# Softmax begun inside the position network, weights loaded early into one room, and layer 1's gathers re-timed, in a four-layer vision kernel

## The chip, the cores and the metric

One core of a Trainium2 chip runs the whole program. TensorE (PE) multiplies; VectorE (DVE), ScalarE (ACT) and GpSimd (POOL) do the rest; SyncE (SP) issues most of the transfers and POOL the gathers. Each engine takes its own instructions strictly in order. The metric is the device time of one execution in microseconds (us). [...]

## What is computed

Two images `x` of 512 channels and 32 x 32 pixels go through four layers, all in float32:

```
# layer 0: attention with 64 sampled keys a group, and a position network
off  = tanh(pw(gelu(dwconv6x6(q)))) * 4           # 8x8 sampling offsets
kv   = grid_sample(xn, grid + off);  k, v = kw(kv), vw(kv)
bias = w3 . relu(w2 . relu(w1 . signed_log(pos)))  # for each query, key
attn = softmax(q k^T / 8 + bias)                   # 8 groups, 1024 x 64
x    = x + out_w(attn v);   x = x + mlp_w2 gelu(mlp_w1 bn(x))
# layer 1: deformable 3x3 convolution as a gate
d    = instance_norm(pw(dwconv3x3(x1)));  off = conv3x3(d)
dc   = deform_conv(d, off)                         # 9 taps, bilinear
x    = x * (d * sigmoid(layer_norm(dc))) + x * g(channel pools of x2)
# layer 2: linear attention;  x = x + gamma * Q (K V) / norm
# layer 3: group norm, attention of 8 heads over 1024 pixels, projection
x    = x + w_out(softmax(q k^T / 8) v)
```

## The kernel before

`layers` runs the stages one after the other, and weaves neighbours together with Python generators: a `yield` is a place where another stage's instructions may be put. PE's instructions stay in the order in which the program issues them (`manual_schedule`); the order on DVE, ACT, POOL and SP is made by the scheduler of the Tile framework. Tiles come from pools of a fixed number of buffers; a new tile in a buffer waits for the last reader of the old one, and so do pools that come to lie where a closed pool lay.

**Layer 0.** `queries_keys_values` ends with the queries in `q_pad`, keys in `kbd`, values in `vbd`. `biased_scores` (L755 to 885) runs the position network for eight pairs of groups, four of each image, two keys at a time: `hidden` (L794, L803) makes the first layer on DVE and ACT, `second_layer` issues matmuls of 32 columns in four column tiles (L814) with their evictions `lo` and `hi` on ACT (L824, L826) and a sum on DVE (L827), and `last_layer` (L835) adds keys into a score tile `sim`, one step behind. At the sixteenth key `scores` adds q times k; `store` (L857) copies a finished pair to `simT`. The score matrices thus sit transposed in `simT`.

`softmax_values` (L888) takes one image. Of each of its four pairs it transposes the scores (L899, pt), takes the maximum, subtracts (L905, L907, DVE), the exponential (L908, ACT), the sum, its reciprocal, the product (L910 to L912, DVE); `values` transposes back (L918, pb) and copies to SBUF (L924, `at`, ACT); `product` multiplies by the values (L930, po) and copies to `simT` (L933, DVE). Before the change image 0's runs alone on PE after the position network, with four two-bank PSUM tiles. `project` (L949) follows, then `Mlp.run(0)`, into which image 1's softmax is woven, and `project` for image 1.

**MLP.** `run` (L984) does two halves of 512 pixels in 16 steps each, ph (L1016), gelu on ACT (L1024), acc (L1005) two steps behind; `acc` is added to `x_all` on DVE (L1033). Its weights of 4 MB each and out_w are loaded when the pools of the position network have closed.

**Layer 1.** Beside `Mlp.run(1)` image 0's features are made (`Features`): x_pad copies on ACT (L1074), nine depthwise steps dw on DVE (L1082, L1086) for each of two halves, a channel gate, pd, then offsets. `Products` makes nine tap tables: 72 tiles of 8 matmul halves each (L1281, py), copied on ACT (L1289, y, four buffers) and written to DRAM by SP (L1290, `table<-y`). `Samples` gathers, for each tap and 128 pixels, the four neighbours (1 MB a tile, two indirect transfers on POOL, L1333) and adds them, weighted, in four DVE instructions (L1344, dfacc). `due` takes a tile when its tap's table is whole. `pools` is the ring of gather buffers; its length also says how many gathers run ahead of the additions. `FOUND` and `MADE` set which MLP step issues what.

After the MLP the rest of image 0's products goes with image 1's features and more of image 0's sums (`sums0`), then image 1's 72 products with: the last of `sums0`, image 0's gate (`gate_image`), image 1's sums (`sums1`), and from the gate on `Linear.run(0)` (layer 2: pqk, pv L1455, v L1463, pkv L1448, pa L1514) and `group_norm_terms` (pm, pvar L1554), one step of these for each product. Then h is normalized (L1612), keys and queries of image 0 are computed (L1652, pq), image 1's gate is woven into their end, and `Linear.run(1)` is woven with `att.values(0)` (32 matmul steps, pv L1629).

**Layer 3.** `heads` (L1705 and after) makes logits (L1719, pl), a maximum (L1807, DVE), an exponential (L1815, ACT), transposes (L1769, pt) and weighted sums (L1734, po) for 64 pieces of work, with one piece ahead, and fills gaps with other steps (`fill`).

## Time and profile before

| what | us |
|---|---|
| median of 3 runs | 4014.14 (4012.45 to 4018.51) |
| the profiled execution's own time | 4015.97 |
| its span, first to last instruction | 4014.2 |
| PE busy in the span | 3895.0 (97%) |
| DVE, ACT, POOL busy | 2980.4, 2530.8, 339.3 |
| mean granted PE clock | 0.992 |
| transfers in the span | 274.39 MB |
| idle on DVE's sums, waiting for gathers | 214.0 in 92 waits |

A stage can be found by its windows on PE: 73.3 us busy in the first 100 us, 8.99, 11.41 and 16.37 us busy in 2100 to 2120, to 2140 and to 2160 (softmax of image 0; clock 0.90, 0.76, 0.83; DMA share 0.76, 0.50 and 0), 92.97 in 2900 to 3000, 96.03, 92.73, 97.05 and 91.83 in the four hundreds that follow, and 31.64 in the 40 us from 3480 on (start of the heads). In the slices of the page each digit is a tenth of busy time in 100.4 us; PEclk is the granted clock. In rows by time the first number is the start and the second the length from first to last of the group (xcount); in brackets stands the idle time of the engine just before, and what ended it. A float32 matmul shows as two instructions. In the list of waits the three numbers are the total, how many, and the longest.

### The profile page before, as it was taken

Reading aid. Unit: us, or ns where it says so; the run is one execution under the profiler, and the core shown is the slowest. Engines: PE = TensorE matmul, PEld = TensorE weight load, DVE = VectorE, ACT = ScalarE, POOL = GpSimd, SP = SyncE. Lnnn points to the kernel's source line nnn. Section 1 sums busy time; section 2 is a strip of 40 time slices with the busy share of each in tenths; the row PEclk is TensorE's granted clock in tenths of the full one; section 3 lists DMA queues with packets and bytes.
Section 4 is the critical chain, followed back from the end, with each engine's and each line's share of the span. In section 5 each row is a group of like instructions: output and inputs, shape, how many; then the busy total and the mean of one; then the engine's idle time right before and its main releaser. Section 6 shows DMA issues by size and latency. Waiting matters only on the chain. (4 is left out here: it accounts for less than half of the span.)

```text
span 4014.2 us, 59880 instructions
## 1 busy us (share of the span) xinstructions
PE 3895.0 (97%) x25548; PEld 1499.3 (37%) x25548; DVE 2980.4 (74%) x3326; ACT 2530.8 (63%) x2848; POOL 339.3 (8%) x325
## 2 busy tenths in 40 slices
PE   7999999999999999999997999999999999999999
PEld 4322222222222222222323444444434344355555
DVE  7999999999999999999983104054768677466665
ACT  7999999999999999999991112111112112155544
POOL 0000000000000000000000000033445343000000
PEclk9999999999999999999998999999999999999999
DMA  3000000000000000000002000166779685000000
GB/s 105 8 15 22 22 22 1 22 22 22 22 1 22 22 22 22 1 22 22 1 9 97 0 0 24 36 217 222 271 268 366 233 325 186 0 1 11 1 19 24
DMA packets 90479, 274.39 MB, mean 68 GB/s; under 512 B 9140, under 2 KB 10804, under 8 KB 86884
## 3 DMA queue, kind: packets, MB, share of 16 engines
q0 software_dynamic: 42432, 154.39, 11.0%
q1 hardware_dynamic: 47780, 116.18, 8.0%
q8 instruction: 200, 3.28, 0.3%
q14 instruction: 67, 0.55, 0.0%
HBM read 228.33 MB, written 42.21 MB: 67 GB/s over the span
## 5 line engine op out<-in xcount | busy, mean ns | idle before, releaser
L814 PE MATMUL ph<-h,w_t 128*32 128x512 f32 x16384 | 1796.0, 593 | 15.5 <-ACT lo L824 7.1
L794 DVE TENSOR_TENSOR h<-ab 128x1024 f32<-128x1024 f32 x1024 | 1206.4, 1220 | 73.5 <-PE ph L814 72.5
L814 PEld LDWEIGHTS ph<-h,w_t 128*32 128x32 f32 x16384 | 530.2, 110 | 1255.9 <-issue 1072.8
L803 ACT ACTIVATE h<-h 128x1024 f32<-128x1024 f32 x832 | 870.0, 1065 | 46.2 <-DVE h L794 43.4
L827 DVE SCALAR_TENSOR_TENSOR hi<-lo,low_w,hi 128x1024 f32<-128x1024 f32 x512 | 655.4, 1280 | 30.0 <-ACT hi L826 29.3
L826 ACT ACTIVATE hi<-ph,size_b,size 128x1024 f32<-128x1024 f32 x512 | 620.1, 1211 | 15.3 <-PE ph L814 9.5
L824 ACT ACTIVATE lo<-ph,vec_t 128x1024 f32<-128x1024 f32 x512 | 570.9, 1115 | 2.4 <-PE ph L814 2.4
L1344 DVE SCALAR_TENSOR_TENSOR dfacc<-got,wts,dfacc 128x512 f32<-128x512 f32 x560 | 409.3, 749 | 210.6 <-DMA got<-table,idx 198.2
L1281 PE MATMUL py<-dc_w_t,d 128*128 128x512 f32 x1152 | 515.5, 601 | 21.2 <-ACT y L1289 21.0
L1289 ACT COPY y<-py 128x512 f32<-128x512 f32 x144 | 83.5, 584 | 502.2 <-PE py L1281 424.4
L1333 POOL DMA_INDIRECT got<-table,idx x288 | 318.6, 1106 | 516.3 <-DVE dfacc L1344 157.6
L1281 PEld LDWEIGHTS py<-dc_w_t,d 128*128 128x128 f32 x1152 | 217.4, 192 | 302.0 <-issue 266.6
L1815 ACT ACTIVATE e<-pl,m 128x1024 f32<-128x1024 f32 x128 | 143.5, 1121 | 226.2 <-DVE m L1807 226.2
L1807 DVE TENSOR_REDUCE m<-pl 128x1 f32<-128x1024 f32 x128 | 150.8, 1220 | 144.5 <-PE pl L1719 144.5
L835 PE MATMUL sim<-hi,w 128*32 128x512 f32 x2048 | 244.8, 592 | 1.8 <-DVE hi L827 1.8
L1016 PE MATMUL ph<-xn,mlp_w_t 128*128 128x512 f32 x512 | 229.6, 593 | 0.0
L1005 PE MATMUL acc<-h,mlp_w_t 128*128 128x512 f32 x512 | 229.4, 592 | 0.0
L1024 ACT ACTIVATE h<-ph,vec_t 128x512 f32<-128x512 f32 x64 | 44.0, 687 | 254.2 <-PE ph L1016 254.0
L1069 POOL MEMSET x_pad<- 128x1156 f32 x2 | 2.2, 1094 | 2061.9 <-PE ph L814 2061.9
L1769 PE MATMUL pt<-cst_t,e 128*128 128x128 f32 x1024 | 147.8, 277 | 5.8 <-ACT aT L1780 3.0
L1769 PEld LDWEIGHTS pt<-cst_t,e 128*128 128x128 f32 x1024 | 117.6, 141 | 92.6 <-issue 61.2
L1005 PEld LDWEIGHTS acc<-h,mlp_w_t 128*128 128x128 f32 x512 | 97.3, 190 | 121.9 <-issue 121.6
(228 smaller groups left out, 2536.9 us busy)
## 6 DMA issues: line engine op xcount, KB each, us to landing
table<-y SPq DMA_DIRECT2D x144, 256.0 KB
ab<-feat_d SPq DMA_DIRECT2D x64, 512.0 KB
dc_w_t<-in_dc_w_dram SPq DMA_DIRECT2D x18, 1024.0 KB
mlp_w_t<-in_mlp_w_dram SPq DMA_DIRECT2D x2, 4096.0 KB
got<-table,idx POOLq DMA_INDIRECT x288
w_qkv_t<-in_w_qkv_dram SPq DMA_DIRECT2D x3, 1024.0 KB
out_dram<-x_all SPq DMA_DIRECT2D x12, 256.0 KB
x_all<-in_x_dram SPq DMA_DIRECT2D x4, 512.0 KB
```

The costliest lines, as they stand in the source:

```text
L794: nc.vector.tensor_tensor(h1, at_x[:, k : k + 1, :].to_broadcast([128, 32, 32]), at_y[:, k, :].unsqueeze(2).to_broadcast([128, 32, 32]), A ...
L803: nc.scalar.activation(h1, h1, AF.Relu)
L814: nc.tensor.matmul(ph[32 * t : 32 * t + 32, half(n)], lhsT=w2[:, c0 : c0 + 32], rhs=pair[t // 2][:, half(n)], start=True, stop=True, skip_ ...
L824: nc.scalar.activation(lo, phs[0], AF.Relu, bias=b2_lo)
L826: nc.scalar.activation(hi, phs[1], AF.Relu, bias=size_b, scale=size)
L827: nc.vector.scalar_tensor_tensor(hi, lo, low_w, hi, ALU.mult, ALU.add)
L835: nc.tensor.matmul(sim[32 * t : 32 * t + 32, half(n)], lhsT=w3[:, 30 - j : 62 - j], rhs=sums[t][:, half(n)], start=(j == 0), stop=(j == 30 ...
L1005: nc.tensor.matmul(accs[oc], lhsT=self.w2[:, m, 128 * oc : 128 * oc + 128], rhs=hs[m], start=(m == 0), stop=(m == 15),)
L1281: nc.tensor.matmul(py, lhsT=f.d[:, cc, 128 * c : 128 * c + 128], rhs=w[:, cc, :], start=(cc == 0), stop=(cc == CC - 1),)
L1333: nc.gpsimd.indirect_dma_start(out=g[:, 2 * dy : 2 * dy + 2, :].rearrange("p s c -> p (s c)"), out_offset=None, in_=self.products.tables[f ...
L1344: self.net.nc.vector.scalar_tensor_tensor(acc, g[:, s, :], self.f.wts[:, c, k, s : s + 1], self.f.bias if (k, s) == (0, 0) else acc, ALU.mult,
L1769: nc.tensor.transpose(pt[:, 128 * c : 128 * c + 128], e[:, 128 * k : 128 * k + 128], ident)
```

## The change

It has six parts.

1. **Room.** `q_pad` becomes the first use of one tile, `room`, of 128 x (4 x 2048 + 2048) floats. After the scores of the last pair the room is taken again, for out_w and the first MLP weight, which `load_weights` loads from there on. `kbd` and `w2` move to a pool of their own. The second MLP weight is loaded where it was.
2. **Softmax of image 0** is called inside `biased_scores`. Its first two steps (transposes, maximum, subtraction and exponential, sum, product of pairs 0 and 1) are issued before the last `last_layer`; the rest comes after it, and the store of pair 7 last. Its PSUM tiles come from the position network's three, its e and at from the buffers of h1 and hi. For image 0 the copy of the product to `simT` goes to ACT instead of DVE.
3. **End of the MLP.** `sums0` has three buffers instead of two, and in MLP steps 30 and 31 no tile of `sums0` is issued.
4. **Layer 1.** The further pool `df_more` has one buffer instead of two. Image 1's features start after the second product. `sums1` has two buffers until image 0's gate is done, and then four more; it had three, and two more from that gate to product 62. The gate takes two steps for each product, Linear and group norm one in two of three products.
5. **Values of image 0.** Only as many steps run beside `Linear.run(1)` as that has; the remaining ones run in `heads` between the first logits and the first transposes, in banks of layer 3.
6. `h1` is a flat tile; `turn` takes a pool and a tag.

Context lines are cut where they do not matter.

```diff
@@ -280,7 +280,8 @@
     def turn(name):
-        return banks["turn"].tile([128, 512], F32, name=name, tag="turn")
+        pool, tag = banks["turn"]
+        return pool.tile([128, 512], F32, name=name, tag=tag)
     bn = 1.0 / math.sqrt(1.0 + 1e-5)
@@ -291,44 +292,64 @@
         vbd = sim_pool.tile([128, NP, 128], F32, name="vbd", tag="vbd")
+        room = ExitStack()
+        big = net.pool(room, "l0_q")
+        def new_room():
+            return big.tile([128, 4 * 2048 + CC * C], F32, name="room", tag="room")
         with ExitStack() as l0a:
             l0a.enter_context(net.tc.manual_schedule(engines={mybir.EngineType.PE}))
-            big = net.pool(l0a, "l0_q")
-            q_flat = big.tile([128, (NP * 36 + 6) * 34], F32, name="q_pad", tag="q_pad")
+            q_flat = new_room()[:, : (NP * 36 + 6) * 34]
             q_pad = q_flat[:, : NP * 36 * 34].rearrange("p (n y x) -> p n y x", y=36, x=34)
-            kbd = big.tile([128, NP, 128], F32, name="kbd", tag="kbd")
+            keys = net.pool(l0a, "l0_k")
+            kbd = keys.tile([128, NP, 128], F32, name="kbd", tag="kbd")
             dram = net.pool(l0a, "cpb_dram", space=bass.MemoryType.DRAM)
             feat = dram.tile([32, 2048], F32, name="feat_d", tag="feat_d")
-            w2 = big.tile([128, 128], F32, name="w2_t", tag="w2")
+            w2 = keys.tile([128, 128], F32, name="w2_t", tag="w2")
             first = net.pool(l0a, "cpb_ab", 4)
...
             nc.sync.dma_start(out=w2, in_=net.ins["w2"])
-            biased_scores(net, q_pad, kbd, feat, w2, simT, first, parts)
+            def load_weights():
+                t = new_room()
+                w1 = t[:, : 4 * 2048].rearrange("p (k m) -> p k m", m=2048)
+                out_w = t[:, 4 * 2048 :].rearrange("p (k m) -> p k m", m=C)
+                nc.sync.dma_start(out=out_w, in_=net.ins["out_w"])
+                nc.sync.dma_start(out=w1, in_=net.ins["mlp_w1"])
+                return w1, out_w
+            w1, out_w = biased_scores(
+                net, q_pad, kbd, feat, w2, simT, vbd, first, parts, load_weights
+            )
         later.enter_context(net.tc.manual_schedule(engines={mybir.EngineType.PE}))
...
         image0 = ExitStack()
-        with ExitStack() as l0b:
-            mlp = Mlp(net, l0b, s2)
-            out_w = net.load("out_w", net.pool(scores, "out_w", side="right"))
+        with room, ExitStack() as l0b:
+            mlp = Mlp(net, l0b, s2, w1)
             soft = net.pool(scores, "att_tmp", 2, side="right")
-            with ExitStack() as ctx:
-                ps = net.psum(ctx, "att_ps", 4)
-                for _ in softmax_values(net, 0, simT, vbd, soft, ps):
-                    pass
             mlp.open_psum(l0b)
...
                 ps = net.psum(ctx, "att_ps1", 1)
+                def two_banks(name):
+                    return ps.tile([128, HW], F32, name=name, tag="two")
+                def one(name, size):
+                    return soft.tile([128, size], F32, name=name, tag=name)
                 project(net, 0, simT, out_w, mlp.bank)
-                weave(mlp.run(0), softmax_values(net, 1, simT, vbd, soft, ps), 1, 3)
+                weave(mlp.run(0), softmax_values(net, 1, simT, vbd, one, two_banks), 1, 3)
                 project(net, 1, simT, out_w, mlp.bank)
...
             with ExitStack() as ctx:
-                banks["turn"] = net.psum(ctx, "ft_ps", 2)
+                banks["turn"] = net.psum(ctx, "ft_ps", 2), "turn"
                 found = f0.run(turn, False)
@@ -336,18 +357,19 @@
                         some(found, 99)
-                        sums0 = Samples(net, f0, products, own0, 2, side="right")
+                        sums0 = Samples(net, f0, products, own0, 3, side="right")
                         taken = sums0.run()
...
                             next(made)
-                            if taken is not None:
+                            if taken is not None and i < 30:
                                 sums0.due(taken)
...
             kv_bank = net.bank(l1, "l2_kv")
-            banks["turn"] = net.psum(l1, "l1_y", 2)
+            banks["turn"] = net.psum(l1, "l1_y", 2), "turn"
             def bank(name):
@@ -357,39 +379,42 @@
             f1 = Features(net, 1, own1)
-            more = net.pool(own1, "df_more", 2)
-            sums0.pools += [more, more]
+            more = net.pool(own1, "df_more", 1)
+            sums0.pools += [more]
             found = f1.run(bank, True)
             for i, _ in enumerate(made):
-                some(found, 2)
+                if i > 1:
+                    some(found, 2)
                 if i % 4 < 3:
...
             sums1 = Samples(net, f1, products, own1, 1)
-            sums1.pools += [more, more]
+            sums1.pools += [more]
             tmp = net.pool(own1, "df_tmp", 1)
...
             taken1 = sums1.run()
-            aside = None
+            aside, ctx2 = None, None
             for i, _ in enumerate(made):
-                if i == 62:
-                    sums1.pools = sums1.pools[:3]
                 if aside is None:
...
                         wait = i + 4
-                else:
-                    sums1.due(taken1)
-                    if i >= wait and next(aside, None) == "gated":
-                        own0.close()
-                        ctx2 = ExitStack()
-                        extra = net.pool(ctx2, "df_extra", 2, side="right")
-                        sums1.pools += [extra, extra]
-                        linear.open(ctx2, side="right")
-                        aside = chain(
-                            linear.run(0, bank, kv_bank),
-                            group_norm_terms(net, linear.tmp, 0, bank),
-                        )
+                    continue
+                sums1.due(taken1)
+                if ctx2 is None and i >= wait:
+                    if next(aside) != "gated" and next(aside) != "gated":
+                        continue
+                    own0.close()
+                    ctx2 = ExitStack()
+                    linear.open(ctx2, side="right")
+                    extra = net.pool(own1, "df_extra", 4)
+                    sums1.pools += [extra] * 4
+                    aside = chain(
+                        linear.run(0, bank, kv_bank),
+                        group_norm_terms(net, linear.tmp, 0, bank),
+                    )
+                elif ctx2 is not None and i % 3 < 2:
+                    next(aside, None)
             for _ in aside:
@@ -409,9 +434,11 @@
                 linear.open(ctx)
-                weave(linear.run(1, bank, kv_bank), att.values(0, turn))
+                values = att.values(0, turn)
+                for _ in linear.run(1, bank, kv_bank):
+                    next(values)
             l2.close()
-        layer3(net, att, later, out)
+        layer3(net, att, later, values, banks, out)
@@ -752,7 +779,9 @@
     return done
-def biased_scores(net, q_pad, kbd, feat, w2, simT, first, parts):
+def biased_scores(net, q_pad, kbd, feat, w2, simT, vbd, first, parts, load_weights):
@@ -790,9 +819,9 @@
             k = 16 * (j // 32) + j % 16
-            h1 = hid1.tile([128, 32, 32], F32, name="h1", tag="h1")
+            h1 = hid1.tile([128, HW], F32, name="h1", tag="h1")
             nc.vector.tensor_tensor(
-                h1,
+                h1.rearrange("p (y x) -> p y x", x=32),
                 at_x[:, k : k + 1, :].to_broadcast([128, 32, 32]),
@@ -801,7 +830,7 @@
                 nc.scalar.activation(h1, h1, AF.Relu)
-            return h1.rearrange("p y x -> p (y x)")
+            return h1
         def second_layer(pair):
@@ -880,18 +909,34 @@
                 scores(p, sim)
+                if p == NP - 1:
+                    weights = load_weights()
             pending = (p, j, sums)
+        def two_banks(name):
+            return ps_h.tile([128, HW], F32, name=name, tag="ph")
+        def one(name, size):
+            if size == HW:
+                pool, tag = (hid1, "h1") if name == "e" else (highs, "hi")
+                return pool.tile([128, HW], F32, name=name, tag=tag)
+            return small.tile([128, size], F32, name=name, tag=f"soft_{name}", bufs=2)
+        soft = softmax_values(net, 0, simT, vbd, one, two_banks)
+        some(soft, 2)
         last_layer(sim, *pending[1:])
+        for _ in soft:
+            pass
         store(NP - 1, sim)
-def softmax_values(net, b, simT, vbd, tmp, ps):
+        return weights
+def softmax_values(net, b, simT, vbd, one, banks):
     nc = net.nc
     ident = net.cst("ident")
-    def banks(name):
-        return ps.tile([128, HW], F32, name=name, tag="two")
     def attention(p):
@@ -901,12 +946,12 @@
             )
-        m = tmp.tile([128, 16], F32, name="m", tag="m")
+        m = one("m", 16)
         nc.vector.tensor_reduce(m, pt, AX.X, ALU.max)
-        e = tmp.tile([128, 16, 64], F32, name="e", tag="e")
+        e = one("e", HW).rearrange("p (h j) -> p h j", j=64)
         nc.vector.tensor_tensor(e, pt, m.unsqueeze(2).to_broadcast([128, 16, 64]), ALU.subtract)
         nc.scalar.activation(e, e, AF.Exp)
-        s = tmp.tile([128, 16], F32, name="s", tag="s")
+        s = one("s", 16)
         nc.vector.tensor_reduce(s, e, AX.X, ALU.add)
@@ -920,7 +965,7 @@
             )
-        at = tmp.tile([128, HW], F32, name="at", tag="at")
+        at = one("at", HW)
         nc.scalar.copy(at, pb)
@@ -930,7 +975,8 @@
             )
-        nc.vector.tensor_copy(simT[:, p, :], po)
+        (nc.scalar.copy, nc.vector.tensor_copy)[b](simT[:, p, :], po)
     first = CC * b
@@ -967,12 +1013,12 @@
     LAG = 2
-    def __init__(self, net, ctx, s2):
-        self.net, self.s2 = net, s2
+    def __init__(self, net, ctx, s2, w1):
+        self.net, self.s2, self.w1 = net, s2, w1
         w = net.pool(ctx, "mlp_w")
...
         self.hp = net.pool(ctx, "mlp_h", self.LAG + 2)
-        self.w1, self.w2 = net.load("mlp_w1", w), net.load("mlp_w2", w)
+        self.w2 = net.load("mlp_w2", w)
     def open_psum(self, ctx):
@@ -1702,7 +1748,7 @@
         self.ps_o = net.psum(ctx, "l3_out", 1)
-    def heads(self, work, fill):
+    def heads(self, work, first, fill):
@@ -1750,6 +1796,8 @@
             self.divide(*e)
+        for _ in first:
+            pass
         for at, (b, hp, s0) in enumerate(work):
@@ -1823,7 +1871,8 @@
         return self.ps_t.tile([128, 512], F32, name=name, tag="pt3")
-def layer3(net, att, ctx, out):
+def layer3(net, att, ctx, values, banks, out):
     att.open_heads(ctx)
@@ -1859,7 +1908,8 @@
     ]
-    att.heads(first + second, fill)
+    banks["turn"] = att.ps_t, "pt3"
+    att.heads(first + second, values, fill)
     for _ in att.project(1, 768, 256, out, att.last_bank):
```

## Prediction

> **What bounds the kernel now.** I read the page first: busy time by engine, then the span in 40 slices.
>
> ```profile
> PE 3895.0 (97%) x25548; PEld 1499.3 (37%) x25548; DVE 2980.4 (74%) x3326; ACT 2530.8 (63%) x2848; POOL 339.3 (8%) x325
> ...
> PE   7999999999999999999997999999999999999999
> ...
> PEclk9999999999999999999998999999999999999999
> DMA  3000000000000000000002000166779685000000
> ```
>
> TensorE (PE) is the bound: 3895.0 of 4014.2 us, so only 119.2 us of the span are idle on it, and 26.7 of those lie in the first 100 us (73.3 us busy there), which the change leaves alone. At most about 92 us of gaps, and the slow matmuls after them, are open to it. No matmul is removed, so every gain has to be a gap. The second dip (slice 22, also in the clock) is the softmax of image 0; the DMA row shows where tables and gathers run. The waits of PE say who opens the gaps:
>
> ```profile
> PE py L1281 <- ACT y L1289: 21.0, 10, 8.7
> PE pb L918 <- DVE e L912: 14.1, 2, 9.0
> ...
> PE pq L1652 <- ACT h L1612: 7.3, 1, 7.3
> ...
> PE pkv L1448 <- DVE v L1463: 5.6, 2, 4.5
> ...
> PE pl L1719 <- ACT e L1815: 2.6, 1, 2.6
> ```
>
> (Total, number, longest.) Four of these five sit where the diff works; now each stage in time.
>
> **Softmax of image 0.** PE, start and length, wait in brackets; then the ACT load of the exponential's table:
>
> ```profile
> 2099.41 4.89 PE L814 MATMUL ph<-h,w_t 128*32 128x512 f32 x42
> ...
> 2110.32 1.94 PE L899 MATMUL pt<-cst_t,simT 128*128 128x128 f32 x16 [1.47 <-DVE simT L857]
> 2121.21 1.97 PE L918 MATMUL pb<-cst_t,e 128*128 128x128 f32 x8 [8.95 <-DVE e L912]
> 2124.27 3.78 PE L930 MATMUL po<-at,vbd 128*128 128x512 f32 x4 [1.10 <-ACT at L924]
> ...
> 2139.78 1.87 PE L918 MATMUL pb<-cst_t,e 128*128 128x128 f32 x8 [5.18 <-DVE e L912]
> ...
> 2152.03 3.27 PE L956 MATMUL po<-simT,out_w_t 128*128 128x512 f32 x7 [1.32 <-DVE simT L933]
> ```
>
> ```profile
> 2115.00 1.28 ACT L908 ACT_TABLE_LOAD   x1 [9.43 <-DVE e L907]
> ```
>
> From the last position-network matmul (2104.3) to the first of the projection (2152.0) go 47.7 us. DVE is the limit: maximum, subtract, sum and product of a pair take 1.22 us each, reciprocal 0.24, so about 5.1 us a pair. ACT: exponential 1.06, copy 1.01.
>
> The new order puts the 16 transposes of pairs 0 and 1 ahead of the last score matmuls, in banks that are free, with nothing between them and 2104.3. In us after 2100: pt0 to 5.4, pt1 to 6.4; DVE m0 to 6.7, the last hi (1.28, now behind m0) to 8.0; scores to 9.9; e0 to 9.2, m1 to 10.4; exponential 0 at 9.3 to 10.35, since the table load no longer waits for DVE and goes into ACT's idle time after the last hi (2105.6); s0 to 11.6, e1 to 12.8, reciprocal, the store of pair 7 (1.28) to 14.4, product of e0 to 15.6. pb0 starts at 15.7 instead of 21.2: a lead of 5.5, after a PE gap of 5.8. Then pb0 1.97, copy 1.1, po0 3.78, pt2 1.91, pb1 1.08 to 25.6. m2 waits for pt2; e2, exponential, s2, m3, e3 and the product of e2 follow to 33.8, so pb2 starts at 33.9 after a gap of 4.1 (before: 39.8 after 5.18). With pb2, po2 slow (1.87, 3.78) and pb3, po3 fast, plus copies, the projection starts at 46.1; with both fast (1.08, 1.98), at 43.4. The stores of the products move from DVE (1.23) to ACT (about 1.0): no loss. Gain 5.9 to 8.6.
>
> [...] The rows: after 8.95 us of waiting, pb, po and pt took 1.97, 3.78 and 1.91 against 1.08, 1.98 and 1.04 when warm, 3.56 us lost; after 5.18, 2.6 lost. [...] by the rows, 46.1 (gain 5.9). I take **7**.
>
> **The loads.** out_w (1 MB) and the first MLP weight (4 MB) overlay the queries after the scores of pair 7 at about 1980, on SP's queue: the last ab loads are already ahead of them, behind them stands only the second MLP weight, which still starts at 2104. The DMA row is 0 there. The projection waited for simT and not for the load, so this buys nothing by itself; it is worth 0 even without cover, because 5 MB are needed 120 us later. The second weight alone (4 MB; 313 GB/s were moved in 2100 to 2120, so 13 us) lands before 2120. Image 0's weights and POOL's clearing of x_pad now wait for the last e of the softmax (about 2134); behind them on SP and POOL stand only tables and gathers, which start over 200 us later (DMA row): 0.
>
> **End of the MLP.** Gathers (POOL), sums (DVE) and tables (PE, ACT, SP) meet here. PE, ACT, DVE and POOL rows:
>
> ```profile
> 2873.61 6.73 PE L1281 MATMUL py<-dc_w_t,d 128*128 128x512 f32 x11 [8.66 <-ACT y L1289]
> ```
>
> ```profile
> 2872.03 1.05 ACT L1074 COPY x_pad<-x_all 128x1024 f32<-128x1024 f32 x1 [10.83 <-DVE dw L1086]
> ```
>
> ```profile
> 2858.90 0.75 DVE L1344 SCALAR_TENSOR_TENSOR dfacc<-got,wts,dfacc 128x512 f32<-128x512 f32 x1 [3.82 <-DMA got<-table,idx]
> ```
>
> PE stood 8.66 us because the y copies are queued on ACT behind the second x_pad copy, that waits for nine DVE steps on the first, and these wait behind a sum whose gather is late. With 1.01 us just before and 1.6 of half clock (11 matmul halves in 6.73 us; 8 take 3.70), 11.3 us are at stake. The change asks for 5 gathers fewer in the last two MLP steps (62 for 72), gives the sums a third buffer, and starts image 1's features two products later: 10 products of 3.43 us stand ahead of the block instead of 9, 34 us, against a second x_pad copy that I put 27 to 32 us after the first product. The gap closes or shrinks to some us. The bias row b_q now stands on DVE ahead of 12 sums (9 us) and waits for the last hidden matmul, about 2822; they still end before the x_all additions at 2843.8, so hidden. Gain 0 to 11, I take **8**. The five tiles come later: 5 x 3.3 us (a tile's 1 MB at the DMA's full share) = 16 us more for the tail.
>
> **Layer 1 and 2 of image 0.** Linear work goes into two of three products instead of each, three products earlier; so 5 instead of 16 products are left after its last statistics. Gaps that this can close: 5.6 (v behind sums) and 1.9 (pvar). Gain 0 to 7, **4**. h no longer waits for gathers into the extra pool; but the 7.3 was the last table's write, which stays: **1**. Against it: image 1's sums have two buffers (three before) until the gate of image 0 is done, then six (five, three at the end). A tile then takes a gather (3.3) and four additions (3.0) in a two-deep ring; some 11 tiles at about 1 us more, with the 16 us above, less what six buffers win back while the table work flows more evenly. The sums ended at 3370.6; the gate of image 1 reaches PE at 3383.9, so some 9 us are free. Between -3 and +9, I take **+3**. The third projection weight (1 MB) now waits for the last gather instead of 3278; it is needed at about 3402, 28 us after 3370.6 + 3.3, and nothing behind it on SP is wanted before the heads: hidden.
>
> **Heads.**
>
> ```profile
> 3483.17 1.99 PE L1719 MATMUL pl<-qk 64*128 64x512 f32 x8
> 3487.76 4.41 PE L1719 MATMUL pl<-qk 64*128 64x512 f32 x8 [2.61 <-ACT e L1815]
> ```
>
> Thirteen value steps (26 halves of 0.44 = 11.5 us) move behind the first logits, over the first exponentials: the 2.61 and the 2.42 of half clock go. Here 2.6 us of idleness were already enough: [...] by the row it is 5.0, and the row decides. The first logits now wait up to 2 us for an addition. Gain 2 to 6, **4**.
>
> **Sum.** -7 - 8 - 4 - 1 + 3 - 4 = -21 against the profiled execution's 4015.97 (span 4014.2 and 1.8 around it): 3995; that execution lies 1.8 over the median of 4014.14, so **3993**.
>
> **Rivals.** (a) Layer 1 stays even: what leaves the MLP's end comes back as later stalls, and only softmax and heads count, -11: 4003. For it: DMA share 0.93 in 2840 to 2870, 0.92 in 3000 to 3100; fewer gathers early are more later. (b) All gaps close: 9 + 11 + 7 + 6 for h + 6 = -39: 3975. For it: all those waits are orders, not bandwidth; against it, h's is a write. (c) It does not do what it says: DVE's 5 us a pair still set the softmax (gain 3), and a new ACT queue before the products and the wait at the logits take most of the rest: about 4009. (d) Slower: the two-buffer ring and the deferred tiles delay the last sum of image 1, and the gate, then Linear, wait on PE one for one. It must eat 9 us of slack, the other gain of 24, and 8 more: 41 us, a dozen tiles at 3.3. For it: additions waited 214 us for gathers in all; a POOL issue took 8.67 us at 2865 while DVE ran without a gap. With 14 tiles (46 us) it is +13: 4027. Against it: POOL stood idle 34 and 24 us near 3201 and 3247 for want of tables, so the tail can catch up.
>
> **How the numbers follow.** Chances: the forecast 0.46 (own range 3984 to 4001), (a) 0.21, (b) 0.15, (c) 0.11, (d) 0.07. A difference of 0.2%, 8 us, is what a measurement can tell from none. Faster: the first three and a third of (c), 0.86; same: most of (c), 0.08; slower 0.06. The range leaves out the low half of (b), and (d): 3975 to 4010.
>
> **What would show it.** pb0 near 2115.7 and the projection at 2143 to 2146; ACT's table load at 2105.6; no wait over 4 us on y near 2873; pkv's wait under 2; second logits in 2 us after a value product. Wrong if PE waits for the gate of image 1; if y's waits move rather than go; or if the first pb still waits for DVE until 2119.

## The result, and the profile after

The changed kernel takes 4001.49 us (median of 6 runs, 3998.97 to 4007.06), the kernel before beside it 4016.29 (4012.45 to 4022.08): 14.8 us less, a ratio of 0.9964 (95% interval 0.9951 to 0.9977). Forecast were 21 us less. The sign, the place of two gains (softmax and heads) and the range were right; the end of the MLP was not.

Four marks on PE divide both profiled executions (4014.2 and 3999.3 us) into stretches that hold the same work: the end of the last position-network matmul, the first of the projection, the last one of the MLP (acc), the first one on h (pq).

| stretch, us | before | after | difference | forecast |
|---|---|---|---|---|
| start to the last position matmul | 2104.3 | 2103.8 | -0.5 | 0 |
| to the projection (softmax of image 0) | 47.7 | 39.4 | -8.3 | -7 |
| to the MLP's last matmul | 687.5 | 687.5 | 0.0 | 0 |
| to the first matmul on h (layer 1, Linear of image 0) | 497.0 | 496.4 | -0.6 | -10 |
| to the end (keys, gate, values, heads) | 677.7 | 672.2 | -5.5 | -4 |

Layer 1's -10 is the sum of -8, -4, -1 and +3 in the prediction. The waits of PE in the page of the changed kernel (total, number, longest):

```profile
PE py L1327 <- ACT y L1335: 26.3, 11, 8.2
...
PE pb L963 <- DVE e L957: 8.9, 2, 5.2
PE pq L1698 <- ACT h L1658: 7.9, 1, 7.9
...
PE pp L1254 <- DVE pos L1201: 4.9, 2, 4.7
```

The waits on v, on the group norm's terms and of the second logits, 5.6, 1.9 and 2.6 before, are gone from the list. The softmax's wait fell from 14.1 to 8.9. But y rose from 21.0 to 26.3, and pos from 0.2 to 4.9. In the order of time, the softmax on PE:

```profile
2103.74 1.97 PE L944 MATMUL pt<-cst_t,simT 128*128 128x128 f32 x16
...
2114.44 1.94 PE L963 MATMUL pb<-cst_t,e 128*128 128x128 f32 x8 [5.19 <-DVE e L957]
2117.48 3.78 PE L975 MATMUL po<-at,vbd 128*128 128x512 f32 x4 [1.10 <-ACT at L969]
2121.05 1.74 PE L944 MATMUL pt<-cst_t,simT 128*128 128x128 f32 x8
2122.64 1.04 PE L963 MATMUL pb<-cst_t,e 128*128 128x128 f32 x8
2124.77 1.98 PE L975 MATMUL po<-at,vbd 128*128 128x512 f32 x4 [1.10 <-ACT at L969]
2126.59 1.04 PE L944 MATMUL pt<-cst_t,simT 128*128 128x128 f32 x8
2131.34 1.09 PE L963 MATMUL pb<-cst_t,e 128*128 128x128 f32 x8 [3.71 <-DVE e L957]
2133.54 3.78 PE L975 MATMUL po<-at,vbd 128*128 128x512 f32 x4 [1.10 <-ACT at L969]
2137.11 1.91 PE L963 MATMUL pb<-cst_t,e 128*128 128x128 f32 x8
...
2143.21 7.13 PE L1002 MATMUL po<-simT,room 128*128 128x512 f32 x16 [1.10 <-ACT simT L979]
```

The transposes stand ahead of the scores, without a wait, and the two waits for e are still there, shorter. The table load went into ACT's free time: no wait in front of it, at 2105.10 and not at 2115.00.

```profile
2105.10 1.28 ACT L953 ACT_TABLE_LOAD   x1
```

The heads' start: the second logits run in 1.99 us, straight after 11.43 us of value steps.

```profile
3461.05 1.99 PE L1765 MATMUL pl<-qk 64*128 64x512 f32 x8
3462.97 11.43 PE L1675 MATMUL pv<-w_qkv_t,h 128*128 128x512 f32 x26
3474.33 1.99 PE L1765 MATMUL pl<-qk 64*128 64x512 f32 x8
```

The end of the MLP, PE and then ACT:

```profile
2842.43 17.43 PE L1327 MATMUL py<-dc_w_t,d 128*128 128x512 f32 x40 [1.41 <-ACT y L1335]
2868.10 16.63 PE L1327 MATMUL py<-dc_w_t,d 128*128 128x512 f32 x32 [8.24 <-ACT y L1335]
```

```profile
2840.84 1.05 ACT L1120 COPY x_pad<-x_all 128x1024 f32<-128x1024 f32 x1 [6.03 <-POOL x_pad L1115]
...
2866.52 1.05 ACT L1120 COPY x_pad<-x_all 128x1024 f32<-128x1024 f32 x1 [12.86 <-DVE dw L1132]
```

The wait that was to close is 8.24 us; it was 8.66. ACT stood idle for 12.86 us ahead of the x_pad copy, though PE waited for y from 2859.86 on, and began the two y copies queued behind it at 2867.47, right at its end: it took neither out of turn. The granted clock behind the wait was 0.50 here (2868.10 to 2872.00) and before (2873.61 to 2876.50). Count from the MLP's last matmul (2839.5 before, 2830.7 after): the second x_pad copy came at 32.5 before and comes at 35.8; eight products stand ahead of this wait, the block, instead of seven (24 + 40 halves against 48 + 8). A later wait in the same stretch, for the offsets' positions, grew as well:

```profile
2985.57 0.29 PE L1254 MATMUL pp<-cst_t,pos 18*128 18x18 f32 x2 [4.72 <-DVE pos L1201]
```

The -0.6 of this stretch hides two changes. In its first 160 us (2839.5 to 2999.5 before, 2830.7 to 2990.7 after) PE is idle for 16.7 us before and 22.6 after; in the rest, for 21.5 before and 15.4 after. So about 6 us were lost near the end of the MLP and about 6 won behind it.

### The profile page after: what moved, and what is told of

The parts are those of the page before. It is cut to its first block, busy times and chain, and to the rows that moved or that the text cites. A ratio compares the mean times of both kernels' runs of the same rounds, so it can differ in the third digit from the quotient of the medians.

```text
span 3999.3 us, 60180 instructions
## 1 busy us (share of the span) xinstructions
PE 3891.3 (97%) x25548; PEld 1497.1 (37%) x25548; DVE 2970.3 (74%) x3322; ACT 2533.9 (63%) x2852; POOL 368.9 (9%) x325
## 3 DMA queue, kind: packets, MB, share of 16 engines
q0 software_dynamic: 42432, 154.39, 10.6%
## 4 chain that ended last, share of the span: by engine, by line
PE 80%; ACT 11%; DVE 4%; DMA 3%; issue 2%; POOL 1%; SPq 0%; ACTq 0%; POOLq 0%; DVEq 0%
PE ph L843 35%; PE py L1327 9%; PE ph L1062 5%; PE acc L1051 5%; PE sim L864 4%; ACT h L832 3%; PE pl L1765 3%; PE po L1780 3%; PE pq L1698 3%; PE pt L1817 3%; ACT hi L855 2%; ACT lo L853 2%; DMA got<-table,idx 2%; ACT ab L473 2%; PE pv L1675 1%
## 5 line engine op out<-in xcount | busy, mean ns | idle before, releaser
L843 PE MATMUL ph<-h,w_t 128*32 128x512 f32 x16384 | 1796.1, 593 | 15.4 <-ACT lo L853 7.0
L856 DVE SCALAR_TENSOR_TENSOR hi<-lo,low_w,hi 128x1024 f32<-128x1024 f32 x512 | 654.6, 1278 | 27.8 <-ACT hi L855 27.1
L1327 PE MATMUL py<-dc_w_t,d 128*128 128x512 f32 x1152 | 519.9, 606 | 26.3 <-ACT y L1335 26.3
L1379 POOL DMA_INDIRECT got<-table,idx x288 | 348.6, 1211 | 458.1 <-DMA table<-y 139.7
L1062 PE MATMUL ph<-xn,room 128*128 128x512 f32 x512 | 229.6, 592 | 0.0
```

The source lines that it names most:

```text
L843: nc.tensor.matmul(ph[32 * t : 32 * t + 32, half(n)], lhsT=w2[:, c0 : c0 + 32], rhs=pair[t // 2][:, half(n)], start=True, stop=True, skip_ ...
L856: nc.vector.scalar_tensor_tensor(hi, lo, low_w, hi, ALU.mult, ALU.add)
L1062: nc.tensor.matmul(ph, lhsT=self.w1[:, k, 128 * m : 128 * m + 128], rhs=xn[:, k, :], start=(k == 0), stop=(k == CC - 1),)
L1327: nc.tensor.matmul(py, lhsT=f.d[:, cc, 128 * c : 128 * c + 128], rhs=w[:, cc, :], start=(cc == 0), stop=(cc == CC - 1),)
```

## The experiments

Ratios are to runs of the kernel before on the same chip, whose median differed (4016 to 4023 us) between the three sittings. Layer 1's stretch is that of the table. It varies between executions of one order: with the changed order of layer 1 it was 496.4, 498.8, 494.8 and 500.0 us in four profiles, 497.5 on average, and start_now and start_again, which are one kernel, differ by 6.0. So a single difference of up to some 6 us in this column tells nothing. The other two columns vary less: with the changed softmax 38.5 to 40.8, with the changed heads 672.1 to 674.7.

| kernel | median us | ratio (95%) | softmax | layer 1 | to the end |
|---|---|---|---|---|---|
| layer1_old | 4007.82 | 0.9965 (0.9951 to 0.9978) | 40.7 | 501.7 | 673.3 |
| heads_old | 4008.32 | 0.9972 (0.9964 to 0.9980) | 39.5 | 498.8 | 677.4 |
| soft_late | 4007.63 | 0.9969 (0.9957 to 0.9980) | 42.1 | 494.8 | 673.0 |
| linear_each | 4006.11 | 0.9964 (0.9950 to 0.9977) | 38.5 | 501.2 | 672.1 |
| xpad_dve | 4005.12 | 0.9958 (0.9944 to 0.9971) | 40.8 | 497.9 | 674.5 |
| xpad_border | 4007.99 | 0.9963 (0.9949 to 0.9976) | 39.5 | 506.2 | 672.3 |
| start_now | 4000.25 | 0.9944 (0.9931 to 0.9958) | 39.5 | 492.9 | 672.1 |
| again | 4003.82 | 0.9969 (0.9957 to 0.9981) | 39.6 | 500.0 | 672.1 |
| start_again | 3992.50 | 0.9936 (0.9922 to 0.9949) | 38.5 | 486.9 | 674.4 |
| start_late | 4002.07 | 0.9959 (0.9945 to 0.9973) | 40.8 | 493.9 | 674.7 |

**First sitting: one part undone at a time.**

layer1_old:

```diff
-                        sums0 = Samples(net, f0, products, own0, 3, side="right")
+                        sums0 = Samples(net, f0, products, own0, 2, side="right")
-                            if taken is not None and i < 30:
+                            if taken is not None:
-            more = net.pool(own1, "df_more", 1)
-            sums0.pools += [more]
+            more = net.pool(own1, "df_more", 2)
+            sums0.pools += [more, more]
-                if i > 1:
-                    some(found, 2)
+                some(found, 2)
...
```

> The changed kernel with the old order of layer 1: two gather buffers for image 0's sums and no hold in the last MLP steps, image 1's features started at once, df_more with two buffers, three buffers for image 1's sums and then five, Linear and group norm one step for each product. The room, the early softmax and the heads stay changed. Theory (layer 1's gaps only moved; its whole part is worth about 0.6 us): the time of the changed kernel within 3 us, 3999 to 4005, and from the MLP's last matmul to the first one on h 497 us (changed: 496.4). Rival (layer 1's orders are worth the 10 us of the forecast and something else took them): about 4011.

The ratio is 0.9965, that of the changed kernel. So the whole of layer 1's new order shows no worth in time, to within the 5 us of the interval; a gain of 10 us would have left 0.999, outside it. (The 3999 to 4005 us expected were missed, but the kernel before is 5 us slower on this chip than beside the changed kernel.) PE is idle for 12.9 us in the first 160 us of the stretch and for 23.4 in the rest, against 22.6 and 15.4 in the changed kernel: the old order is better at the end of the MLP and worse behind it. Its stretch, 501.7, is 5 over that of the kernel before with the same order; the pools lie elsewhere since the room came, and the cause was not followed.

heads_old:

```diff
-                for _ in linear.run(1, bank, kv_bank):
-                    next(values)
+                weave(linear.run(1, bank, kv_bank), values)
```

> The changed kernel with all 32 value steps of image 0 beside and behind Linear as before, none in the heads. Theory (the wait for the first exponentials and the half-speed logits come back): 4 to 5 us slower than the changed kernel, about 4006; the second logits take 4.4 us after a wait of 2.6. Rival (the banks shared with the transposes and the wait of the first logits cost what they gain): no difference, 4001.

The end takes 677.4 us, as before the change, against 672.2: 5.2 for this part. (The ratio, 0.9972 with an interval from 0.9964 on, can't tell so little from the changed kernel.) The old pair of rows is back:

```profile
3478.89 1.99 PE L1764 MATMUL pl<-qk 64*128 64x512 f32 x8
3483.49 4.61 PE L1764 MATMUL pl<-qk 64*128 64x512 f32 x8 [2.61 <-ACT e L1862]
```

soft_late:

```diff
-        some(soft, 2)
         last_layer(sim, *pending[1:])
```

> The changed kernel, but the softmax's first transposes are issued after the last score matmuls; banks, the free table load and the copies on ACT stay. Theory (the early start is one of three parts: no wait for the store's bank 1.4, table load off the path 1.3, start ahead of the scores the rest): 44 to 45 us from the last position matmul to the projection (changed 39.4, before 47.7), total about 4006. Rival (the early start is all of it): 47 to 48 us there, total about 4010.

From the last position matmul to the projection 42.1 us: 2.7 more than with the early start, 5.6 less than before. The early start gives about a third of the gain and not all. The rest is left to banks (tiles in PSUM, where PE writes its results), table load and the copies on ACT, which were not undone one by one. Both numbers expected were too high. The first pb starts 14.3 us after the last position matmul (16.9 before, 10.6 changed), so 3.7 of lead at pb become 2.7 at the projection. The 1.0 between them is the speed of the matmuls: after the second wait po and the pb behind it took 3.39 and 1.04 here, 3.78 and 1.91 in the changed kernel (last section), 1.3 us less, of which slower ones ahead of that wait took back 0.3.

linear_each:

```diff
-                elif ctx2 is not None and i % 3 < 2:
+                elif ctx2 is not None:
```

> The changed kernel with Linear and group norm one step for each product instead of two in three. Theory (this spread is the one order in layer 1 that gained): the waits of PE on v and on the group norm's terms come back, 5 to 8 us, total 4006 to 4009. Rival (gaps only move, layer 1 is set by gathers): within 2 us of the changed kernel, and the wait of PE on y or h shorter by what those waits take.

Layer 1 takes 501.2 us, 3.7 over the average of the changed order, which is within its scatter, and the waits of Linear and group norm are back, on PE in this stretch:

```profile
3185.02 1.22 PE L1494 MATMUL pkv<-v,kf 128*64 128x512 f32 x2 [1.78 <-DVE v L1509]
3199.85 1.07 PE L1494 MATMUL pkv<-v,kf 128*64 128x512 f32 x2 [0.41 <-DVE v L1509]
3261.87 0.39 PE L1600 MATMUL pvar<-spread,cst_t 128*128 128x4 f32 x2 [2.46 <-DVE spread L1597]
```

They sum to 4.7 us. But other waits are shorter: behind the first 160 us PE is idle for 17.5 us in all, and for 15.4 to 17.7 in the four profiles of the changed order. The ratio, 0.9964, can't tell a part of that size either. So the spread moved these waits, and a gain of 4 us by it is not shown; the rival fits as well.

**Second sitting: why does the end of the MLP gain nothing?** The first thought was the queue: y copies behind the second x_pad copy on ACT.

xpad_dve:

```diff
-            nc.scalar.copy(
-                x_pad[:, 1:33, 1:33], x[:, b, cc, :].rearrange("p (y x) -> p y x", x=32)
-            )
+            copy = nc.vector.tensor_copy if spread and cc else nc.scalar.copy
+            copy(x_pad[:, 1:33, 1:33], x[:, b, cc, :].rearrange("p (y x) -> p y x", x=32))
```

> The changed kernel with image 1's second x_pad copy on DVE instead of ACT, so that no y copy stands behind it. Theory A (this queue order is what kept the forecast gain at the MLP's end away): the wait of 8.2 on y goes, with its half clock, and layer 1's stretch (last MLP matmul to the first one on h) falls from 496 to about 487; total about 3992. Rival B (gaps only move: what starts earlier waits later for gathers and sums): the stretch stays within 3 us of 496 and the total at 4001.

The wait on y is gone; the stretch stays at 497.9. PE ran 72 halves in a row, came to pd earlier, and stood there for the depthwise steps:

```profile
2845.38 31.17 PE L1326 MATMUL py<-dc_w_t,d 128*128 128x512 f32 x72 [1.38 <-ACT y L1334]
...
2885.80 4.54 PE L1147 MATMUL pd<-dw,pw_w_t 128*128 128x512 f32 x6 [3.18 <-DVE dw L1131]
...
2919.50 0.70 PE L1326 MATMUL py<-dc_w_t,d 128*128 128x512 f32 x1 [3.70 <-ACT y L1334]
```

Rival B: the place of the wait moves, the end of the chain does not; the last transposes of image 1's offsets (pp) come 157.1 us after the MLP's last matmul, in the changed kernel 155.4. Theory A, my own of the queue, fell.

xpad_border (as the last, and):

```diff
-        nc.gpsimd.memset(d_pad, 0.0)
+        for t in (d_pad[:, :, 0, :], d_pad[:, :, 33, :], d_pad[:, :, 1:33, 0], d_pad[:, :, 1:33, 33]):
+            (nc.vector if spread else nc.gpsimd).memset(t, 0.0)
```

> As the one before, and for image 1 the border of d_pad alone is cleared, by DVE, in place of the whole of it by POOL behind the gathers (3.96 us). Theory A: also the waits of 2.8 on y and 4.7 on pos near 2940 and 2985 shrink, 3 to 6 us more: stretch about 483, total about 3988. Rival B: stretch within 3 us of 496.

No gain either (0.9963), and 506.2 us in its profile, with a wait of 6.2 on dw at pd and one of 7.4 on y later. Why this execution is 8 us longer is open.

start_now and start_again are one kernel, again is the changed one:

```diff
-                if i > 1:
-                    some(found, 2)
+                some(found, 2)
```

> The changed kernel with image 1's features started at once instead of after two products. Theory A (two products more before the block are taken back by a second copy that comes later, as its clearing on POOL and the first copy stand behind gathers): the wait on y at the block grows by at most 3 us and the total stays within 3 us of 4001. Rival C (the later start was worth its two products): 7 us slower, 4008.

> The changed kernel once more, to be compared with the next two on the same chip: 0.996 of the kernel before.

> The kernel that starts image 1's features at once, once more. Theory D (the later start costs time: the features of image 1 are the longest chain of layer 1, and a start two products earlier brings its end forward): 4 to 8 us faster than the changed kernel beside it. Rival B (gaps only move, and the first result was chance): within 3 us of it.

Without the later start the kernel is faster: 0.9944 in one sitting (where 4000.25 stands against 4022.98 of before), 0.9936 in the next, where the changed kernel beside it has 0.9969; 3992.50 against 4003.82 us, 11.3 less, more than expected. Theory A and rival C of the first of them, neither of which had a gain over the changed kernel, both fell; theory D holds. On PE and ACT of start_again:

```profile
2839.95 17.43 PE L1326 MATMUL py<-dc_w_t,d 128*128 128x512 f32 x40 [2.20 <-ACT y L1334]
2860.16 10.57 PE L1326 MATMUL py<-dc_w_t,d 128*128 128x512 f32 x24 [2.77 <-ACT y L1334]
...
2915.22 9.58 PE L1326 MATMUL py<-dc_w_t,d 128*128 128x512 f32 x16 [6.38 <-ACT y L1334]
```

```profile
2838.37 1.05 ACT L1119 COPY x_pad<-x_all 128x1024 f32<-128x1024 f32 x1 [13.68 <-POOL x_pad L1114]
...
2858.57 1.05 ACT L1119 COPY x_pad<-x_all 128x1024 f32<-128x1024 f32 x1 [7.39 <-DVE dw L1131]
```

The MLP's last matmul ended at 2830.9. So the x_pad copies come at 7.5 and 27.7 us after it instead of 10.1 and 35.8, the last scaling of d at 84.9 (start_now 83.4) instead of 97.6 (again 96.7), and the last transposes of the offsets, behind which all of image 1's products are queued, at 138.9 (146.9) instead of 155.4 (155.0). The block is a wait of 2.77, and the one on pos 1.63 with three of 0.2 instead of 4.7 (again 7.5). One wait on y near 2915 is 6.38 (start_now 5.29), where the changed kernel has three of 3.62, 1.34 and 2.77. In sum PE is idle for 15.4 us in the first 160 us (start_now 15.8), in the four profiles of the changed order for 20.6 to 24.1; behind them it is idle for 16.0 (17.1), much as there.

start_late (as start_now, and):

```diff
-                if i % 4 < 3:
+                if i > 8 and i % 4 < 3:
                     sums0.due(taken)
```

> As the one before, and image 0's sums are held for the first nine products after the MLP, while image 1's depthwise steps are made, so that no sum that waits for a gather stands ahead of these on DVE. Theory E (sums waiting for gathers on DVE delay the features, and with them the copies on ACT that y waits for): the wait on y near the second x_pad copy goes, the stretch of layer 1 falls by 3 to 8 us. Rival B: the gathers left over come back as waits later, stretch within 3 us of the one before; the nine tiles (30 us) also delay image 0's gate.

It is slower than start_again: 0.9959, 9.6 us. The second x_pad copy comes at 27.7 as there, and the last depthwise step begins at 48.1, not earlier (44.9). So holding back the sums did not bring these steps forward, and theory E fell. A new wait stands where Linear of image 0 ends:

```profile
PE pvar L1599 <- DVE spread L1596: 8.1, 1, 8.1
```

That is 8.1 us of a wait that start_again does not have, almost the whole difference. Just before, DVE worked through 16 additions of sums in a row (12.52 us from 3308.44 on), and the small steps that this matmul needs came behind them. That these are late because of the tiles held back is likely and not shown.

**Gathers alone.** In the changed kernel one gather's issue on POOL took 15.41 us at 2869.46, in the stretch in which DVE alternates depthwise steps and sums. In the kernel before one took 8.67, as the prediction cited; DVE ran two-input steps from 2859.57 to 2873.33 there, and the issue ended 0.83 us later. My theory was that such steps hold the issue up, which two rows alone do not show; two kernels of gathers alone put it to the test.

micro (its core):

```diff
+        order = [[quiet] * 24, [two] * 24, [one] * 36, [two, two, one] * 10, [two_out] * 24]
+        for n, work in enumerate(order):
...
+            for f in work:
+                f()
+            for g in range(8):
+                nc.gpsimd.indirect_dma_start(
```

> A kernel of its own that computes nothing of the reference: five parts, each of eight gathers of 128 x 1024 from a table in DRAM, issued by POOL with a ready index; beside them DVE does nothing; 24 two-input steps of 128 x 1024 (multiply by a scalar and add); 36 one-input steps; two two-input and one one-input step in turn; 24 plain additions of two inputs. Theory S (a gather's issue on POOL stands still while DVE runs two-input steps from SBUF without a pause): about 1 us an issue in the first and third part, in the second one issue that lasts as long as the steps (some 30 us), in the fourth about one in each group of three steps. Rival T (the long issues of the kernel come from a full DMA queue): about 1 us in all parts.

micro2:

```diff
-        order = [[quiet] * 24, [two] * 24, [one] * 36, [two, two, one] * 10, [two_out] * 24]
+        order = [[quiet] * 24, [chained] * 24, [two] * 24, [two] * 12, [two, two, two, two, one] * 5]
```

> As the kernel of gathers alone, but with other parts: DVE does nothing; 24 two-input steps in one chain, each waiting for the one before; 24 two-input steps in two chains in turn, so that none waits for its neighbour; 12 of these; five groups of four such steps and one one-input step. Theory S2 (a gather's issue stands still only while two-input steps follow without the small gap that a chain leaves): about 1 us in the first two parts, one issue as long as the steps in the third (some 28 us) and fourth (some 14 us), about 5 us at most in the fifth. Rival T (the long issues are the DMA queue's): about 1 us in all.

In these kernels theories S and S2 both fell. POOL and DVE in the third part of micro2, with 23 two-input steps following without a gap:

```profile
73.20 1.73 POOL L68 DMA_INDIRECT gots<-table,idx  x1 [21.97 <-DVE idx L64]
75.24 0.94 POOL L68 DMA_INDIRECT gots<-table,idx  x1 [0.30 <-issue]
```

```profile
72.86 27.83 DVE L43 SCALAR_TENSOR_TENSOR b<-a,s,b 128x1024 f32<-128x1024 f32 x23
```

All issues there took 0.93 to 1.73 us. In the other parts of both kernels they lie between 0.93 and 1.80 as well, beside one-input steps at 1.27 to 1.36 being even a little slower.

But the profiles of the full kernel tie the long issues to DVE. POOL and DVE in the changed kernel:

```profile
2869.46 15.41 POOL L1379 DMA_INDIRECT got<-table,idx  x1 [0.81 <-DVE dfacc L1390]
```

```profile
2883.32 0.74 DVE L1390 SCALAR_TENSOR_TENSOR dfacc<-got,wts,dfacc 128x512 f32<-128x512 f32 x1
2888.91 2.08 DVE L1390 SCALAR_TENSOR_TENSOR dfacc<-got,wts,dfacc 128x512 f32<-128x512 f32 x3 [4.85 <-DMA got<-table,idx]
```

From 2869.12 to 2884.06 DVE ran two-input steps without a pause, and the issue ended at 2884.87, 0.81 us later; an issue that nothing holds takes 0.94. The next long one, 11.69 us from 3169.82 on, ends 0.82 us after 17 additions in a row. In the twelve profiles 36 issues took over 4 us, and 35 of them end 0.8 to 0.9 us after a run of such steps ends, at a pause, at a step with one input or at a step that reads PSUM. This is what theory S would look like, held for a whole run of steps. Rival T of a full DMA queue fits worse: the DMA share was 0.62 and then 0.18 in the two halves of the long issue (2869 to 2877, 2877 to 2885).

Such a run is not enough, though. During nine additions in a row of the changed kernel, from 3162.66 on, two issues took 1.02 us each, and in micro2 none was held. What decides whether an issue is caught stays open. Not tried were steps that read the strided x_pad, additions of data just gathered, and gathers already outstanding.

## Why the prediction was right, and where not

- *Softmax, 7 forecast, 8.3 measured.* Every step is in the rows: transposes with no wait, table load off the path, the first pb that waits 10.6 us after the last position matmul (forecast 11.4), the other 27.5 (29.6). The waits left are 5.19 and 3.71 (5.8 and 4.1). Both were followed by slow matmuls, at a granted clock of 0.50 (2114.44 to 2116.38 and 2117.48 to 2121.20; 2133.54 to 2139.00), so the change cured neither. The 7 was an estimate between the 5.9 with slow matmuls also after the second wait and the 8.6 with fast ones there. The first slow stretch cost 0.90 + 1.80 + 0.70 = 3.4 us (pb, po, pt against 1.04, 1.98, 1.04), what the row of before gave (3.56).
- *Loads, 0.* The stretch of 687.5 us is the same to 0.1.
- *End of the MLP, 8 forecast: this step failed.* It said that a later start of the features puts 10 products ahead of the block instead of 9, and that the second x_pad copy still comes 27 to 32 us after the first product. There were 8 instead of 7: one more, as said, but I had counted the two products that wait in PSUM twice. And the copy's time is not independent of the start: with the later start it came at 35.8, without it at 27.7, so the start's delay of the copy was put at nothing and was 8 us. The later start cost about 11 us by the timing and 7.6 by the stretch (497.5 against the mean of 492.9 and 486.9). What the later start delays is the chain of image 1's features (x_pad, dw, pd, statistics, d, d_pad, offsets, pos), and the waits of PE along it say where PE meets that chain. Its end moves the stretch, but not one for one: the last transposes came 8.5 and 16.5 us earlier in start_now and start_again than in the changed kernel, the stretch was 3.5 and 9.5 shorter. Before the change they came at 145.9, 9.5 us earlier than in the changed kernel, and the stretch was no shorter, since more was waited for behind them. I read the wait as a fault of ACT's queue; xpad_dve showed that without this queue it turns up at pd. The line that I had named as a sign of error, "if y's waits move rather than go", is what happened. With an early start the kernel reached 3992.50 and 4000.25 us in two sittings; the 3993 of the forecast is in reach of it, and not of the changed one.
- *Hold and third buffer* were part of the same 8. They did not bring the second x_pad copy forward: layer1_old, which has neither and starts at once, has it at 27.8. In all else they are not told apart. Against 492.9 and 486.9 for the early start, layer1_old has 501.7; it differs in these two, in image 1's buffers, in the gate's steps and in Linear's order, and which of them wins the 6 us behind the first 160 us is open.
- *Linear spread, 4 forecast.* The waits of 5.6 and 1.9 are gone, and undoing it brought 4.7 back; but PE's idle time behind the first 160 us stayed in its scatter, so the gain is not shown. *h, 1 forecast:* 7.9 instead of 7.3, nothing.
- *Tail, +3.* PE did not wait for image 1's gate, nor for the third projection weight. The rival that ends slower had no sign in any run. The 3.3 us of a tile is near the 3.36 at which the gathers of six tiles follow one another in before (3076.68 to 3096.82, DMA share 1.01), and somewhat high for 1 MB alone: at the 346 GB/s of 3000 to 3100, where the DMA share was 0.92, that takes 3.0.
- *Heads, 4 forecast, 5.5 measured,* 5.2 of it by undoing the part. The second logits of before took 4.41 us at a granted clock of 0.61, those of the changed kernel 1.99 at 1.00.

So layer 1 stayed even, as rival (a) had it, with 4003 for it and 4001.5 measured. Its mechanism is not what happened: the gap at the MLP's end never closed, and what the later start lost was won back behind it by orders that the forecast had priced apart. That the two came out equal is chance. The sums for softmax and heads were right and slightly low.

## What to carry to other kernels

When an engine waits at several places along one stage, look for the chain that those places share before giving each wait a price: a wait that is removed at one place comes back at the next if the chain ends as late as before. The sooner start of the features' chain was worth 7.6 us by the stretch and 11.3 by the timing, about as much as the largest gain of the change itself (8.3, the softmax). And move a step that fills a gap only with the count of what stands ahead of it in each queue, PSUM banks included, since both counts and the time of the blocking instruction change together.

## What the runs showed of the hardware

The clock after one and the same wait differs between executions. The code of the softmax is the same in after, xpad_dve and linear_each, and so are its waits, 5.19 and 3.71. In after the pb behind the second wait took 1.09 at a granted clock of 1.00, and po then 3.78 at 0.50. In linear_each pb took 1.09, po 3.41 and the two behind them 1.04 and 1.98, and in xpad_dve pb itself took 1.97. The stretch was thus 38.5 to 40.8 us long, so one wait of 3.71 had a price from 1.5 us (linear_each: 0.05 + 1.43) to 3.6 (xpad_dve: 0.93 + 1.80 + 0.88). The mean granted clock from that pb to the projection was 0.84 in linear_each, 0.71 in after and 0.66 in xpad_dve. What decides in which of the matmuls behind a wait the clock falls is not shown. Gathers were issued beside DVE steps with two inputs from SBUF at 0.93 to 1.80 us each in the kernels of gathers alone; in the full kernel single ones took up to 15.41 us, and nearly all of the long ones ended 0.8 to 0.9 us after a run of such steps.
